# Inverse roots on GpSimd, and degree scaling folded into the adjacency, in a four-layer graph network kernel

## The chip, the cores and the metric

The kernel runs on one core of a Trainium2 chip. The core has five engines with queues of their own: TensorE (PE in the profile, with its weight loads as PEld), VectorE (DVE), ScalarE (ACT), GpSimd (POOL) and SyncE (SP), which here only issues DMAs. Each engine takes its instructions in order. The metric is the device time of one execution in microseconds; the median of three runs of the kernel before is 5732.73 us (5721.88 to 5733.99).

## What is computed

There are 64 graphs of 256 nodes with 128 features and a 0/1 adjacency. Each goes through four layers, and after each layer the input is added and the rows are normalised (mean and variance over the features).

```python
# layer 0: p[i] + q[j] + b, relu, masked by the adjacency, maximum over j
# layer 1: three elu projections, two aggregations with adj and adj^T, tanh of a linear map
# layer 2
A_hat = adj + eye;  deg = A_hat.sum(-1);  dinv = where(deg > 0, rsqrt(deg), 0)
norm_A = dinv[:, None] * A_hat * dinv[None, :]
h = elu(elu(x @ W0 + b0))
h = elu(norm_A @ (h @ W1) + b1)
out = norm_A @ (h @ W2) + b2
# layer 3: for every edge (i, j): layernorm(m_j + m_i + b1), exact gelu, summed over j,
#          then a linear map, a layernorm with gain and bias
x = layernorm(x + layer(x))          # after each of the four
```

Inverse square roots occur in three places: in every layernorm (five per graph, one value for each node), in `dinv` (one value for each node), and in layer 3, where each edge has its own variance and so its own inverse root.

## The kernel before

A graph's 256 nodes lie on the partitions in two halves (H = 2 tiles of 128 rows). Layers 0 and 3 work on edges. The kernel sorts the nodes by degree and packs the edges into "slots" of falling width; the `WIDTH` columns of a half are cut into five tiles of up to 1024 columns (`TILES`), so that one graph has ten edge tiles in layer 3 (`TODO`).

Four stages form a software pipeline over the graphs: `first` (the packing and layer 0), `second` (layer 1), `third` (layer 2, then the first four edge tiles of layer 3) and `last` (the rest of layer 3 and the output). In each of 67 steps, `together` interleaves four stages of four successive graphs: the stages are Python generators, and a `yield` is a point at which another stage may put its instructions in. The order on each engine then comes from the framework's scheduler, which starts from this order and moves instructions by their dependencies and by its own costs. All 64 graphs are unrolled. A second path, `general`, is built behind a run-time test and isn't executed with these inputs.

The lines that matter here:

- `inverse_root` (L72 to L75): a ScalarE square root in place, then a VectorE reciprocal in place. It has three users.
- `Shared.layernorm` (L166): VectorE takes statistics (L171, L172) and adds the epsilon (L174); after a `yield` the root follows, after another the normalisation (L180, or L184 and L185).
- `Shared.layer_2` (L261): it takes the degrees, adds one, makes the mask `pos` and the root `dinv` (L265 to L274), and adds the identity to the transposed adjacency `aT` (L277). In each of its two aggregation steps VectorE multiplies the features `hs` by `dinv` (L293, one instruction per half), TensorE multiplies by `aT` (L296), ScalarE copies (L299), TensorE applies the weights (L304), and L308 multiplies the result's rows by `dinv` and adds the bias.
- `sums_of` (L718), for each edge tile: TensorE gathers (L728), VectorE adds (L732), ScalarE squares (L736), TensorE sums over the features (L743), ScalarE scales into `row` with the epsilon (L745), and a DMA writes `row` to a `line` in DRAM (L750). For each two tiles a DMA brings `line` back spread over the partitions as `vr` (128 or 108 partitions by 16, L762), another brings the mask `fu` (L764); `vr` gets its inverse root (L768) and is multiplied by the mask (L769), and a DMA writes it to DRAM as `scale_line` (L771).
- `last` fetches each tile's scales, broadcast to all partitions, as `rs_s` (L828, two tiles ahead), multiplies with them (L839), applies Gelu (L841) and folds the result into `sums` (L492).
- All DMAs are issued from SP's one queue. A DMA in it that waits for an engine holds back the DMAs behind it.
- ScalarE holds one set of activation functions at a time; the built program has a table load (ACT_TABLE_LOAD, put down to the line of the activation behind it) where the next function isn't in the set that is loaded. Sqrt, Exp and Gelu alternate in this kernel. Copy, Square, Identity, Sign and others need no load.

Of the kernel before, what the change touches and what calls it, by code (L numbers as in the profile page):

```python
# [9 lines left out]
F32 = mybir.dt.float32  # L10
BF16 = mybir.dt.bfloat16
AF = mybir.ActivationFunctionType
ALU = mybir.AluOpType
# [6 lines left out]
P = 128  # L20
EPS = 1e-5
# [22 lines left out]
def kernel(  # L44
# [9 lines left out]
    nc = tc.nc  # L54
    B, N, D = x.shape
    assert N == 2 * P and D == P
    H = N // P
    Q = P // 4

    consts = ctx.enter_context(tc.tile_pool(name="consts", bufs=1))  # L60
# [6 lines left out]
    eps_t = consts.tile([P, 1], F32, name="eps_t")  # L67
    nc.vector.memset(eps_t, EPS)
    minus1 = consts.tile([P, 1], F32, name="minus1")
    nc.vector.memset(minus1, -1.0)  # L70

    def inverse_root(t):  # L72

        nc.scalar.activation(t, t, AF.Sqrt)  # L74
        nc.vector.reciprocal(t, t)  # L75

    def load(src, shape, name):
        t = consts.tile(shape, F32, name=name)
# [43 lines left out]
    with tc.tile_pool(name="prep", bufs=1) as prep, tc.tile_pool(  # L122
        name="ps_prep", bufs=2, space=bass.MemoryType.PSUM
# [33 lines left out]
    class Shared:  # L157
# [8 lines left out]
        def layernorm(self, dst, src, g=None, be=None):  # L166

            st = self.work.tile([P, H, 6], F32, name="st", bufs=4)
            mv = self.work.tile([P, H, 2], F32, name="mv", bufs=4)
            for h in range(H):  # L170
                nc.vector.bn_stats(st[:, h], src[:, h])  # L171
                nc.vector.bn_aggr(mv[:, h], st[:, h])  # L172
            rs = self.work.tile([P, H], F32, name="rs", bufs=4)
            nc.vector.tensor_scalar(rs, mv[:, :, 1], EPS, None, ALU.add)  # L174
            yield
            inverse_root(rs)
            yield
            for h in range(H):
                if g is None:
                    nc.vector.tensor_scalar(  # L180
                        dst[:, h], src[:, h], mv[:, h, 0:1], rs[:, h:h + 1], ALU.subtract, ALU.mult
                    )
                else:
                    nc.vector.scalar_tensor_tensor(dst[:, h], src[:, h], mv[:, h, 0:1], g, ALU.subtract, ALU.mult)  # L184
                    nc.vector.scalar_tensor_tensor(dst[:, h], dst[:, h], rs[:, h:h + 1], be, ALU.mult, ALU.add)  # L185
# [17 lines left out]
        def to_features(self, xn, name, bufs=None):  # L203

            pt = self.psum()
            for h in range(H):
                nc.tensor.transpose(pt[:, h * P:(h + 1) * P], xn[:, h], ident)
            t = self.state.tile([P, N], F32, name=name, **({"bufs": bufs} if bufs else {}))
            nc.scalar.copy(t, pt[:, :N])
            return t  # L210

        def node_tile(self, name):
            return self.state.tile([P, H, P], F32, name=name)
# [44 lines left out]
            yield from self.layernorm(x2, y)  # L258
            s["x2"] = x2

        def layer_2(self, s, aT, deg_of):  # L261

            work, psum, elu = self.work, self.psum, self.elu
            x2 = s["x2"]
            deg = work.tile([P, H], F32, name="deg")  # L265
            deg_of(deg)
            nc.vector.tensor_scalar(deg, deg, 1.0, None, ALU.add)
            pos = work.tile([P, H], F32, name="pos")
            nc.vector.tensor_scalar(pos, deg, 0.0, None, ALU.is_gt)
            dinv = work.tile([P, H], F32, name="dinv")  # L270
            nc.vector.tensor_scalar(dinv, deg, 1e-30, None, ALU.max)
            inverse_root(dinv)
            yield
            nc.vector.tensor_mul(dinv, dinv, pos)  # L274
            for h in range(H):
                blk = aT[:, h, h * P:(h + 1) * P]
                nc.vector.tensor_add(blk, blk, ident)  # L277
            yield
            xT = self.to_features(x2, "xT_2", 1)
            yield  # L280
            ph = psum()
            hs = work.tile([P, H, P], F32, name="hs")
            for h in range(H):
                cols = slice(h * P, (h + 1) * P)
                nc.tensor.matmul(ph[:, cols], xT[:, cols], w2[0], start=True, stop=True)
            yield
            for h in range(H):
                nc.vector.tensor_add(hs[:, h], ph[:, h * P:(h + 1) * P], b2[0])
            yield from elu(hs, hs, twice=True)
            yield  # L290
            for step in (1, 2):
                for h in range(H):
                    nc.vector.tensor_scalar(hs[:, h], hs[:, h], dinv[:, h:h + 1], None, ALU.mult)  # L293
                pa = psum()
                for h in range(H):
                    nc.tensor.matmul(pa[:, :N], hs[:, h], aT[:, h], start=h == 0, stop=h == H - 1)  # L296
                yield
                agg = work.tile([P, N], F32, name="agg")
                nc.scalar.copy(agg, pa[:, :N])  # L299
                yield  # L300
                po = psum()
                for h in range(H):
                    cols = slice(h * P, (h + 1) * P)
                    nc.tensor.matmul(po[:, cols], agg[:, cols], w2[step], start=True, stop=True)  # L304
                yield
                hs = work.tile([P, H, P], F32, name="hs")
                for h in range(H):
                    nc.vector.scalar_tensor_tensor(  # L308
                        hs[:, h], po[:, h * P:(h + 1) * P], dinv[:, h:h + 1], b2[step], ALU.mult, ALU.add
                    )  # L310
                if step == 1:
                    yield from elu(hs, hs)
                yield
            nc.vector.tensor_add(hs, hs, x2)
            x3 = self.node_tile("x3")
            yield from self.layernorm(x3, hs)
            s["x3"] = x3
# [36 lines left out]
    def sparse(ctx):  # L354
# [35 lines left out]
        with tc.tile_pool(name="cs_prep", bufs=1) as pp:  # L390
            t = pp.tile([P, P], F32, name="upto_f")
# [4 lines left out]
            t = pp.tile([P, N], I32, name="iota_i")  # L396
            nc.gpsimd.iota(t, pattern=[[1, N]], base=0, channel_multiplier=0)
            nc.vector.tensor_copy(iota_k, t)
            t = pp.tile([P, 1], I32, name="part_i")
# [25 lines left out]
            t = pp.tile([P, 1], F32, name="gbe")  # L425
# [9 lines left out]
            for i in range(3):  # L435
                t = pp.tile([3, P], BF16, name="u_part")
# [5 lines left out]
            t = pp.tile([ROWS, g_n, g_w], F32, name="tail_f")  # L442
# [7 lines left out]
        state = ctx.enter_context(tc.tile_pool(name="state", bufs=2))  # L450
        hold = ctx.enter_context(tc.tile_pool(name="hold", bufs=4))
        pair = ctx.enter_context(tc.tile_pool(name="pair", bufs=1))
        work = ctx.enter_context(tc.tile_pool(name="work", bufs=1))
        big = ctx.enter_context(tc.tile_pool(name="big", bufs=2))
        sh = Shared(work, state, ps_mm)
# [46 lines left out]
        def first(g, s):  # L502
# [37 lines left out]
            nc.scalar.activation(diff, diff, AF.Abs, accum_out=fl[:, 0:1])  # L540
            kc = work.tile([P, H, H], F32, name="kc")
            nc.vector.scalar_tensor_tensor(kc, pc, -1.0, down_c, ALU.mult, ALU.subtract)
            dg = state.tile([P, H], F32, name="dg", bufs=3)
            nc.vector.tensor_reduce(dg, pc, AX.X, ALU.add)
            s["dg"] = dg

            more = work.tile([P, H, H], F32, name="more")
            for h in range(H):
# [169 lines left out]
        def sums_of(s, i):  # L718

            h, t0, tl = TODO[i]  # L720
# [45 lines left out]
                s["fulls"].rearrange("h w -> (h w)")[first_at:first_at + n].rearrange("(p k) -> p k", k=PIECE),  # L766
            )
            inverse_root(vr[:rows])  # L768
            nc.vector.tensor_mul(vr[:rows], vr[:rows], fu[:rows])  # L769
            out_line = dram.tile([1, GROUP * TILE], F32, name="scale_line")  # L770
            nc.sync.dma_start(out_line[:, :n].rearrange("o (p k) -> (o p) k", k=PIECE), vr[:rows])  # L771
            at = 0
# [8 lines left out]

        def third(g, s):

            dg = s["dg"]

            def deg_of(deg):
                nc.vector.tensor_scalar(deg, dg, 1.0 / N, None, ALU.mult)

            yield from sh.layer_2(s, s["aT"], deg_of)
            yield  # L790
            x3, perm = s["x3"], s["perm"]

            x3T = sh.to_features(x3, "x3T")
            yield
            pc = psum()
            for h in range(H):
                nc.tensor.matmul(
                    pc[:, h * N:(h + 1) * N], x3T[:, h * P:(h + 1) * P], w3c.rearrange("p c o -> p (c o)"),
                    start=True, stop=True,
                )  # L800
            pcv = pc.rearrange("p (h c o) -> p h c o", h=H, c=2)
            dn = work.tile([P, H, P], F32, name="dn")
            nc.scalar.copy(dn, pcv[:, :, 1])
            c3 = state.tile([P, 3, H, P], BF16, name="c3")
            split3(c3, pcv[:, :, 0])
            yield
            pd = psum()
            for h in range(H):
                for hi in range(H):
                    nc.tensor.matmul(  # L810
                        pd[:, h * N:(h + 1) * N], dn[:, hi], perm[:, h, hi], start=hi == 0, stop=hi == H - 1
                    )
            yield
            dT = state.tile([P, H, N], F32, name="dT")
            nc.scalar.activation(dT, pd.rearrange("p (h n) -> p h n", h=H), AF.Identity, bias=b3c)
            s.update(x3T=x3T, c3=c3, dT=dT)
            yield
            for i in range(AHEAD):
                yield from sums_of(s, i)
# [75 lines left out]
    def general(ctx):  # L895
# [82 lines left out]
        def middle(g, s):  # L978
# [7 lines left out]
                nc.scalar.copy(aT[:, hj], pt[:, :N])  # L986
            yield

            def deg_of(deg):
                nc.vector.tensor_reduce(deg, an, AX.X, ALU.add)  # L990

            yield from sh.layer_1(s, an, aT, s["x1"])
            yield
            yield from sh.layer_2(s, aT, deg_of)
            yield

            x3T = sh.to_features(s["x3"], "x3T")
# [145 lines left out]
```

## Time and profile before

| | busy us | share of the span | instructions |
|---|---|---|---|
| TensorE matmul | 4529.9 | 79% | 27408 |
| VectorE | 4834.4 | 84% | 14654 |
| ScalarE | 4275.2 | 75% | 6485 |
| GpSimd | 1.9 | 0% | 10 |

The profiled execution took 5731.62 us, and its span is 5729.7 us; its mean granted TensorE clock is 0.862 of full speed. The table loads of ScalarE are groups of their own: 535 before Gelu (L841), 445 before Sqrt (L74), 221 and 32 before Exp (L194, L198), two before Tanh (L254) and one in the preamble (L426), each 1283 ns. The DMA engines are busy for about a fifth of the span.

A row of a group names line, engine and operation, output and inputs, shapes, count, then busy time in all and mean duration of one, then the engine's idle time just ahead of these instructions and what ended it. The chain is followed back from the last instruction, at each step to what released it.

### The profile page before, as it was taken

To read this page: it belongs to the slowest core of one execution; us is meant where nothing else is said; L and a number is where in the kernel's file an instruction comes from. 1 tells how busy PE (TensorE), PEld (TensorE's weight loads), DVE (VectorE), ACT (ScalarE), POOL (GpSimd) and SP (SyncE) were. 2 spreads that over 40 slices of the span, in tenths; PEclk is the share of its full clock that TensorE was granted. 3 is DMA by queue.
4 is the path that set the end of the run, shared out by engine and by line. 5 is a ranking of instruction groups with operands and counts; after the bars stand their busy time and mean duration, and the time that the engine had idled before them with its cause. 6 is when DMAs were issued, how large, how long until landed. Compare 5 with 4: busy or idle time off the path is not lost.

```text
span 5729.7 us, 83531 instructions
## 1 busy us (share of the span) xinstructions
PE 4529.9 (79%) x27408; PEld 2508.7 (44%) x27408; DVE 4834.4 (84%) x14654; ACT 4275.2 (75%) x6485; POOL 1.9 (0%) x10
## 2 busy tenths in 40 slices
PE   5878878878778778788788788787887887877875
PEld 2444444444444444444444444444444444444443
DVE  6788888888888888888888888888888888888876
ACT  2577777777777777777777777777777777777785
POOL 0000000000000000000000000000000000000000
PEclk8888889889889889888898898898888887888986
DMA  0122222222212221221221222122212212221222
GB/s 22 44 70 63 62 63 72 62 63 66 69 57 70 65 63 63 72 63 62 63 72 62 63 65 70 59 68 65 63 62 72 64 62 63 69 66 60 68 65 74
DMA packets 292813, 365.15 MB, mean 64 GB/s; under 512 B 151952, under 2 KB 210448, under 8 KB 292368
## 3 DMA queue, kind: packets, MB, share of 16 engines
q1 hardware_dynamic: 292368, 359.73, 20.0%
q8 instruction: 217, 3.56, 0.3%
q14 instruction: 228, 1.87, 0.1%
HBM read 345.07 MB, written 14.53 MB: 63 GB/s over the span
## 4 chain that ended last, share of the span: by engine, by line
PE 52%; DVE 29%; ACT 11%; issue 4%; DMA 3%; SPq 0%; DVEq 0%; POOL 0%; ACTq 0%
PE bigp L665 11%; PE bigp L728 8%; DVE pre L839 6%; PE mm L860 5%; DVE lanes L492 4%; PE mm L743 4%; DVE hot L629 4%; DVE pre L732 4%; DVE sums L492 3%; PE bigp L681 3%; DMA rs_s<-scale_line 2%; PE mm L870 2%; PE mm L296 2%; PE mm L699 2%; PE mm L647 2%
## 5 line engine op out<-in xcount | busy, mean ns | idle before, releaser
L665 PE MATMUL bigp<-hot,q 128*128 128x512 fp8e4 (+1 forms) x3840 | 1052.3, 371 | 66.6 <-DVE lanes L492 52.6
L728 PE MATMUL bigp<-hot,c 128*128 128x512 fp8e4 (+1 forms) x3840 | 928.8, 372 | 140.2 <-DVE pre L732 140.2
L732 DVE TENSOR_TENSOR pre<-bigp,dT 128x512 f32<-128x512 f32 (+6 forms) x1664 | 846.3, 530 | 37.8 <-PE bigp L728 33.5
L492 DVE TENSOR_TENSOR lanes<-bigp,lanes 128x512 f32<-128x512 f32 (+6 forms) x1536 | 772.7, 503 | 94.6 <-PE bigp L681 86.9
L839 DVE TENSOR_TENSOR pre<-pre,rs_s 128x1024 f32<-128x1024 f32 (+1 forms) x640 | 732.9, 1150 | 48.6 <-DMA rs_s<-scale_line 48.0
L736 ACT ACTIVATE sq<-pre 128x1024 f32<-128x1024 f32 (+1 forms) x640 | 638.5, 998 | 169.9 <-DVE pre L732 163.9
L841 ACT ACT_TABLE_LOAD x535 | 686.4, 1283 | 9.5
L492 DVE TENSOR_TENSOR sums<-pre,sums 128x1024 f32<-128x1024 f32 (+6 forms) x1024 | 628.8, 614 | 41.2 <-ACT pre L841 40.7
L745 ACT ACTIVATE row<-mm,eps_t 128x256 f32<-128x256 f32 (+1 forms) x640 | 289.6, 453 | 476.9 <-PE mm L743 476.7
L841 ACT ACTIVATE pre<-pre,be,g 128x1024 f32<-128x1024 f32 (+1 forms) x512 | 594.2, 1172 | 57.8 <-DVE pre L839 53.0
L743 PE MATMUL mm<-sq,ones 128*32 128x256 f32 (+1 forms) x5120 | 482.9, 440 | 135.2 <-ACT sq L736 135.2
L74 ACT ACT_TABLE_LOAD x445 | 570.9, 1283 | 7.5
L728 PEld LDWEIGHTS <-c 128*128 128x128 bf16 x3840 | 331.2, 98 | 550.5 <-issue 136.1
L665 PEld LDWEIGHTS <-q 128*128 128x128 bf16 x3840 | 310.8, 97 | 392.6 <-issue 112.0
L296 PE MATMUL mm<-aT,hs 128*128 128x256 f32 x512 | 232.3, 600 | 316.1 <-DVE hs L293 214.8
L629 DVE TENSOR_SCALAR hot<-rank 128x512 fp8e4<-128x512 bf16 (+5 forms) x1536 | 440.5, 348 | 0.0
L681 PEld LDWEIGHTS <-pick 42*128 42x128 bf16 x2944 | 155.8, 95 | 481.5 <-issue 474.2
L296 PEld LDWEIGHTS mm<-aT,hs 128*128 128x128 f32 x512 | 135.6, 293 | 425.8 <-issue 316.1
L860 PE MATMUL mm<-w3u,sums 128*128 128x128 f32 x2048 | 296.7, 289 | 18.4 <-DVE sums L492 16.1
L194 ACT ACT_TABLE_LOAD x221 | 283.5, 1283 | 3.9
L681 PE MATMUL bigp<-lack,pick 42*128 42x36 bf16 (+16 forms) x2944 | 285.7, 187 | 0.0
L860 PEld LDWEIGHTS mm<-w3u,sums 128*128 128x128 f32 x2048 | 254.5, 195 | 37.3 <-issue 17.6
(226 smaller groups left out, 7132.6 us busy)
## 6 DMA issues: line engine op xcount, KB each, us to landing
rs_s<-scale_line SPq DMA_DIRECT2D x512, 512.0 KB
rs_s<-scale_line SPq DMA_DIRECT2D x128, 352.0 KB
an<-in_adj SPq DMA_DIRECT2D x64, 256.0 KB
x<-in_x SPq DMA_DIRECT2D x64, 128.0 KB
line<-row SPq DMA_DIRECT2D x512, 4.0 KB
out<-o SPq DMA_DIRECT2D x64, 128.0 KB
fu<-fulls SPq DMA_DIRECT2D x192, 4.0 KB
vr<-line SPq DMA_DIRECT2D x192, 8.0 KB
```

The lines of the kernel that those rows point to most:

```text
L74: nc.scalar.activation(t, t, AF.Sqrt)
L492: nc.vector.tensor_tensor(lanes[:, :k, :w], src[:, i:i + k], lanes[:, :k, :w], op)
L629: nc.vector.tensor_scalar(hot[:, :, at:at + w], rank[:, :, :w], s0 + i + 1.0 - FAR, None, ALU.is_equal, saturate=False)
L665: nc.tensor.matmul(pt[:, :tl], q3[:, i, h], hot[:, h, t0:t0 + tl], start=i == 0, stop=False)
L681: nc.tensor.matmul(o_, l_, r_, start=False, stop=i == len(todo) - 1)
L728: nc.tensor.matmul(pt[:, :bl], c3[:, k, h], hot[:, h, t0 + b:t0 + b + bl], start=k == 0, stop=k == 2)
L732: nc.vector.tensor_add(block(pre[:, b:], n, w, at), block(pt, n, w, at), widen(dT[:, h, :w], n))
L736: nc.scalar.activation(sq[:, :tl], pre[:, :tl], AF.Square)
L743: nc.tensor.matmul(pr[q * Q:(q + 1) * Q, :tl // 4], ones[:, :Q], v4[:, :, q], start=True, stop=True)
L839: nc.vector.tensor_mul(pre[:, :tl], pre[:, :tl], rs[:, :tl])
L841: nc.scalar.activation(msg[:, :tl], pre[:, :tl], AF.Gelu, bias=be3, scale=g3)
L860: nc.tensor.matmul(pt[:, cols], lanes[:, k, cols], w3u[:, 1], start=k == 0, stop=False)
```

## The change

- `inverse_root` becomes one GpSimd instruction, a power with exponents from a constant tile `mhalf` of -0.5. Its users are now the edge scales `vr` and `dinv`; the multiplications by the masks that follow (`fu`, `pos`) go to GpSimd too.
- The layernorm has its own root: ScalarE's square root reads the variances directly and adds the epsilon as its bias. The reciprocal moves behind the second `yield`, just ahead of the normalisation.
- `dinv` is made in stage `first`, where the degrees are computed, and kept in a state tile with four buffers; before, the degrees were kept in one with three.
- Layer 2 multiplies the rows of `aT`, with the identity added, by `dinv` once for both aggregation steps. The two multiplications of `hs` in each step go.

```diff
+    mhalf = consts.tile([P, 16], F32, name="mhalf")
+    nc.vector.memset(mhalf, -0.5)
     def inverse_root(t):
-        nc.scalar.activation(t, t, AF.Sqrt)
-        nc.vector.reciprocal(t, t)
+        nc.gpsimd.tensor_tensor(t, t, mhalf[:t.shape[0], :t.free_size()], ALU.pow)
@@ layernorm
+            yield
             rs = self.work.tile([P, H], F32, name="rs", bufs=4)
-            nc.vector.tensor_scalar(rs, mv[:, :, 1], EPS, None, ALU.add)
-            yield
-            inverse_root(rs)
-            yield
+            nc.scalar.activation(rs, mv[:, :, 1], AF.Sqrt, bias=eps_t)
+            yield
+            nc.vector.reciprocal(rs, rs)
@@ new in Shared
+        def inverse_root_of(self, deg, bufs):
+            nc.vector.tensor_scalar(deg, deg, 1.0, None, ALU.add)
+            pos = self.work.tile([P, H], F32, name="pos")
+            nc.vector.tensor_scalar(pos, deg, 0.0, None, ALU.is_gt)
+            dinv = self.state.tile([P, H], F32, name="dinv", bufs=bufs)
+            nc.vector.tensor_scalar(dinv, deg, 1e-30, None, ALU.max)
+            inverse_root(dinv)
+            nc.gpsimd.tensor_mul(dinv, dinv, pos)
+            return dinv
@@ layer_2
-            deg = work.tile([P, H], F32, name="deg")
...
-            nc.vector.tensor_mul(dinv, dinv, pos)
+            dinv = dinv_of()
+            yield
             for h in range(H):
                 blk = aT[:, h, h * P:(h + 1) * P]
                 nc.vector.tensor_add(blk, blk, ident)
+            for h in range(H):
+                nc.vector.tensor_scalar(aT[:, h], aT[:, h], dinv[:, h:h + 1], None, ALU.mult)
...
             for step in (1, 2):
-                for h in range(H):
-                    nc.vector.tensor_scalar(hs[:, h], hs[:, h], dinv[:, h:h + 1], None, ALU.mult)
                 pa = psum()
@@ first
-            dg = state.tile([P, H], F32, name="dg", bufs=3)
+            dg = work.tile([P, H], F32, name="dg")
             nc.vector.tensor_reduce(dg, pc, AX.X, ALU.add)
-            s["dg"] = dg
+            nc.vector.tensor_scalar(dg, dg, 1.0 / N, None, ALU.mult)
+            s["dinv"] = sh.inverse_root_of(dg, 4)
@@ sums_of
             inverse_root(vr[:rows])
-            nc.vector.tensor_mul(vr[:rows], vr[:rows], fu[:rows])
+            nc.gpsimd.tensor_mul(vr[:rows], vr[:rows], fu[:rows])
```

More of the change, by code (lines that the diff above doesn't have):

```diff
@@ L259, in layer_1, with layer_2 @@
             s["x2"] = x2
-        def layer_2(self, s, aT, deg_of):
+        def layer_2(self, s, aT, dinv_of):
             work, psum, elu = self.work, self.psum, self.elu
             x2 = s["x2"]
-            deg = work.tile([P, H], F32, name="deg")
[L266 to L272, printed above, removed]
+            dinv = dinv_of()
             yield
-            nc.vector.tensor_mul(dinv, dinv, pos)
             for h in range(H):
@@ L782, in third @@
         def third(g, s):
[L784 to L789, printed above, removed]
+            yield from sh.layer_2(s, s["aT"], lambda: s["dinv"])
             yield
@@ L987, in middle, with dinv_of @@
             yield
-            def deg_of(deg):
+            def dinv_of():
+                deg = work.tile([P, H], F32, name="deg")
                 nc.vector.tensor_reduce(deg, an, AX.X, ALU.add)
+                return sh.inverse_root_of(deg, 1)
             yield from sh.layer_1(s, an, aT, s["x1"])
             yield
-            yield from sh.layer_2(s, aT, deg_of)
+            yield from sh.layer_2(s, aT, dinv_of)
             yield
```

## The prediction

> **What bounds the kernel now.** I read the busy times first.
>
> ```profile
> PE 4529.9 (79%) x27408; PEld 2508.7 (44%) x27408; DVE 4834.4 (84%) x14654; ACT 4275.2 (75%) x6485; POOL 1.9 (0%) x10
> ```
>
> No engine is full, and three are close to it: the steps are limited by engines that wait for each other in order. The chain of waits says the same.
>
> ```profile
> PE 52%; DVE 29%; ACT 11%; issue 4%; DMA 3%; SPq 0%; DVEq 0%; POOL 0%; ACTq 0%
> ```
>
> TensorE has half of the path, and the change leaves its work alone. VectorE and ScalarE have 40%, and there it cuts. The groups of instructions price what goes.
>
> ```profile
> L841 ACT ACT_TABLE_LOAD x535 | 686.4, 1283 | 9.5
> L74 ACT ACT_TABLE_LOAD x445 | 570.9, 1283 | 7.5
> L194 ACT ACT_TABLE_LOAD x221 | 283.5, 1283 | 3.9
> ...
> L75 DVE RECIPROCAL vr<-vr 128x16 f32<-128x16 f32 (+1 forms) x320 | 78.4, 245 | 29.5 <-ACT vr L74 25.4
> L560 DVE TENSOR_SCALAR perm<-iota_k,place 128x256 f32<-128x256 f32 x256 | 72.7, 347 | 0.1
> L293 DVE TENSOR_SCALAR hs<-hs,dinv 128x128 f32<-128x128 f32 x256 | 61.0, 270 | 2.2
> L769 DVE TENSOR_TENSOR vr<-vr,fu 128x16 f32<-128x16 f32 (+1 forms) x320 | 52.9, 165 | 0.3
> L174 DVE TENSOR_SCALAR rs<-mv 128x2 f32<-128x2 f32 x320 | 51.1, 160 | 0.1
> ```
>
> More than a third of ScalarE's busy time is table loads (1236 of 1283 ns, 1586 us). The timeline of ScalarE in one step shows them alternating where nothing but table switches separates the work:
>
> ```profile
> 3020.31 1.28 ACT L194 ACT_TABLE_LOAD   x1
> 3021.60 0.63 ACT L194 ACTIVATE elu_e<-io 128x512 f32<-128x512 f32 x1
> 3022.25 1.28 ACT L74 ACT_TABLE_LOAD   x1
> 3023.55 0.21 ACT L74 ACTIVATE vr<-vr 108x16 f32<-108x16 f32 x1
> ...
> 3025.36 1.28 ACT L194 ACT_TABLE_LOAD   x1
> ```
>
> A root of 0.21 us costs two loads. Last, the waits at the places that the change touches:
>
> ```profile
> PE mm L296 <- DVE hs L293: 214.8, 67, 8.7
> ...
> DVE pre L839 <- DMA rs_s<-scale_line: 48.0, 57, 4.2
> ```
>
> So the edge scales sometimes arrive just too late, and the layer-2 products wait for VectorE.
>
> **What the Trainium skill says.** "ScalarE: Activation LUTs", section What ACT_TABLE_LOAD costs, gives about 1283 ns for a load of any set; the trace agrees to the digit. "VectorE: DVE Perf Modes", section Mode 2×_2P, says that an fp32 multiplication by a scalar within SBUF takes two elements a cycle through both read ports; the trace agrees: L200 takes 289 ns for 256 columns and 415 ns for 512, so 0.49 ns more per column. "SBUF — State Buffer", section Who interferes with whom, says that the second port pair is shared with GpSimd and locked: a VectorE instruction in such a mode, or with two SBUF inputs, and a GpSimd instruction that reads SBUF exclude each other for a whole instruction. No line of the kernel before shows it, since GpSimd has ten instructions, all in the preamble. This lock is the main risk.
>
> **The change part by part.**
>
> *Table loads and roots on ScalarE.* In the changed program as built, the executed path has 767 loads in place of 1236: Gelu 535 to 379, Sqrt 445 to 195, Exp 253 to 191 (both lines). 469 × 1.283 = 602 us of ScalarE, and 384 roots × about 0.21 = 81 us: 683 us less. On the path, counted by adding the chain's pieces line by line: loads before L74 48.1 us, before L194 89.4, L198 39.7, L841 12.8. Scaled by the share of each that goes (250/445, 32/221, 30/32, 156/535): 27 + 13 + 37 + 4 = 81 us. The roots of `vr` have 8 on it. Together 89.
>
> *VectorE, removed:* reciprocals of `vr` 78.4 and `dinv` 9.4, masks 52.9 and 6.4, epsilon 51.1, L293 61.0: 259 us. *Added:* 128 multiplications of `aT`, 128×256, priced between L200's 289 and L560's 347 ns; I take 320: 41 us. Net 218 us less busy. On the chain stand L174 22, `vr` L75 22, L293 14, L769 10: 68; the addition at VectorE's share of the path (0.29/0.84 = 35%) takes back 14. Net 54.
>
> *The scale's way.* From the issue of the DMA that brings `vr` to the issue of the one that takes `scale_line` away, five groups of one step took 5.73, 8.05, 5.98, 3.73 and 5.18 us, mean 5.73. In the shortest the root began 2.91 us after the issue, right behind a ScalarE copy, so 2.9 is an upper estimate of the DMA. The root, reciprocal and mask take 0.62; the rest, 2.2 us, is queueing behind other work of ScalarE and VectorE. After the change it is 2.9 + power + mask on an engine with nothing else to do. The mask on GpSimd: "GPSIMD Engine Reference", section 3.1, gives 2.6 cycles per element for two inputs at 1.2 GHz, so 16 elements are 0.04 us plus a fixed part; the preamble's GpSimd instructions (386 and 450 ns for 128 and 192 columns) bound it from above; I take 0.2. The power has no price on a page and no row. Below, it can't be under the mask's 0.2. Above: section 7 of the same page gives 4 cycles for each link of a dependent fp32 chain; 20 to 60 links for a logarithm and an exponential (my guess at the number) are 80 to 240 cycles per element, 1.1 to 3.2 us for 16. I take 1.3. Then the way is 4.4 us, 1.3 shorter. The chain runs through `rs_s` DMAs 32 times and `scale_line` DMAs 9 times: 41 × 1.3 = 53 us. With a power of 3.2 it is 23 us longer instead; with 0.2, 100 us shorter.
>
> SP's queue: in the built order `scale_line` comes right behind `vr` in several groups, where before `row` DMAs stood between. SP waits there for GpSimd, and the `row` and `rs_s` issues behind it wait with it; at 4.4 us a group, five groups hold SP for 22 of about 86 us of a step, so I cost it at nothing; at a power over 3 us that cover thins.
>
> *Made in `first`.* `dinv`'s four small VectorE instructions only move, about 40 us of work in both kernels; its root is ready a stage before `aT` needs it. The layernorm's moved reciprocal costs nothing by itself: it stands next to the normalisation, which needs it anyway.
>
> *The port lock.* GpSimd gets 320 × (1.3 + 0.2) + 64 × 0.5 = 512 us of instructions. VectorE work that reads two SBUF tensors or uses two ports: L839 733, `sums` of L492 629, L629 440, and some thirty smaller groups, about 1000: 2800 of 5730 us, 49%. If each GpSimd instruction holds the lock throughout, VectorE loses 512 × 0.49 = 250 us, and at 35% on the path 88 us. If the lock is held only while it reads, next to nothing. I take half, 44.
>
> *Sum.* 89 + 54 + 53 = 196 us off the present path. The step alternates between paths of near length (VectorE's 73 us, TensorE's 71.5 and ScalarE's 65.5 in an 86 us window), so a second one takes over; I keep three quarters, 147. Less 44 of lock: 103 off the profiled execution's 5731.6, so about 5630. The profiled execution and the median of the runs, 5732.7, are 1 us apart, so this holds for the median.
>
> **Rivals.** *GpSimd becomes the brake (slower).* The power takes long and holds the port. With full lock and a power of p us, the balance is −107 (three quarters of 89 + 54) + 0.17 × (320 × (p + 0.2) + 32) + 41 × (p − 2.6); zero at p = 2.1. At 3.2 us it gives +109, so 5840; at 3.6 some 5880. For it: nobody has priced the power, [...]and VectorE is the fullest engine. Against: the tile is only 16 columns. *The relief compounds.* The lock is nothing, and VectorE keeps its 84% at 4616 us of work: 4616 / 0.844 = 5470; with part of it, 5520. For it: ScalarE loses 12% of the span, and it often holds VectorE and TensorE up (L743 waits 135 us for L736, L304 62 us for L299). Against: TensorE's half of the path stays. *Nothing moves.* TensorE's work and the packing's run of L629 take the path wherever it is relieved: 5720 to 5740. Against: loads and `vr` stand on the chain themselves. That the loads don't go can't be: their number is in the built program.
>
> **How the numbers follow.** Likeliest, 5630 (its own range 5550 to 5715): 0.46. Compounding, 5520: 0.14. Brake, around 5840: 0.30. Nothing moves: 0.10. About 0.2% is what a measurement of this kernel can tell. Faster is then 0.46 + 0.14 + 0.02 of the last; same 0.07; slower 0.31. The range drops half of the compounding case and a third of the brake: 5490 to 5880.
>
> **What would show it.** Right: 767 loads and ScalarE near 3600 us busy; VectorE near 4620 plus stretched instructions; `vr` powers of about 1.3 us on GpSimd; L296 waiting less for VectorE; fewer `rs_s` DMAs on the chain. Wrong: powers over 2 us; L839 or L492 `sums` longer than 1216 and 1219 ns at 1024 columns; L839 waiting for `rs_s` far more than 48 us; SP stalled at `scale_line`; a lower granted TensorE clock when its waits shrink.

## The result, and the profile after

The changed kernel takes 5826.45 us, the median of four runs (5820.15 to 5836.14); the kernel before takes 5729.03 us beside it (5721.88 to 5733.99). The ratio is 1.0172 with a 95% interval of 1.0153 to 1.0192: 97 us slower, where 103 us faster was forecast. The time lies inside the range that was given, near the 5840 us of the rival "GpSimd becomes the brake".

The first view is the busy times of the changed kernel, in the same columns as the line shown of the kernel before.

```profile
PE 4572.8 (78%) x27408; PEld 2549.1 (44%) x27408; DVE 4697.2 (81%) x13439; ACT 3683.1 (63%) x5632; POOL 1237.5 (21%) x778
```

The work did go away: ScalarE is 592 us less busy and VectorE 137 us, and the run is longer all the same. The table loads are down to 767, as counted ahead, and no engine is as full as VectorE was. So the loss is mostly waiting, not work. TensorE alone is busier, by 43 us for the same 27408 matmuls, at a mean granted clock of 0.844 against 0.862; what that is worth is looked at below, at the half power. The new work is on GpSimd; its two dearest groups, and the load groups of ScalarE, read:

```profile
L77 POOL TENSOR_TENSOR vr<-vr,mhalf 128x16 f32<-128x16 f32 (+1 forms) x320 | 1025.6, 3205 | 4302.0 <-DMA vr<-line 4302.0
...
L842 ACT ACT_TABLE_LOAD x379 | 486.3, 1283 | 6.7
...
L177 ACT ACT_TABLE_LOAD x195 | 250.2, 1283 | 3.5
...
L196 ACT ACT_TABLE_LOAD x189 | 242.5, 1283 | 3.4
...
L775 POOL TENSOR_TENSOR vr<-vr,fu 128x16 f32<-128x16 f32 (+1 forms) x320 | 151.3, 473 | 25.1
```

One power over 16 columns takes 3205 ns in the mean (shortest 2898, median 2902, longest 3994). The mask takes 217 ns at its shortest, 218 in the median, and 473 in the mean.

Next the waits, in the order engine, waiting line, what released it, then total, number of times and longest. The chain of waits of this kernel can't be used: its chain breaks off at the end of the program.

```profile
PE mm L572 <- DVE perm L566: 365.5, 64, 7.5
DVE pre L840 <- DMA rs_s<-scale_line: 308.0, 87, 5.8
...
DVE rest L503 <- ACT q L502: 187.5, 62, 3.1
```

The second is the change's own: VectorE's multiplication of an edge tile by its scales (L840, L839 before) waits 308 us for them, against 48. The other two are old waits that grew: TensorE's for `perm` was 245.5 us, VectorE's for `q` 93.4 us.

The instructions of VectorE themselves did not get longer. These are its groups of 1024 columns in the changed kernel, the shapes kept apart; both read two tensors in SBUF:

```profile
L840 DVE TENSOR_TENSOR pre<-pre,rs_s 128x1024 f32<-128x1024 f32 x512 | 622.0, 1215 | 297.5 <-DMA rs_s<-scale_line 297.4
...
L497 DVE TENSOR_TENSOR sums<-pre,sums 128x1024 f32<-128x1024 f32 x256 | 311.3, 1216 | 82.5 <-ACT pre L842 82.3
```

They took 1216 and 1219 ns before. Whatever the shared port does, it is not these VectorE instructions that are stretched.

**Where the 308 us lie.** Added up by edge tile over the 64 graphs, 270 us of the wait are at tile 2, in 63 of the 64 graphs; before, tile 2 waited 1.3 us in all, and the largest sum of any tile was 26 us. Tiles 2 and 3 share one group of scales, made at the end of stage `third` and used near the beginning of `last`. From the issue of the DMA that brings this group's `vr` to the issue of the one that takes its `scale_line` away it takes 6.87 us in the mean, against 4.92 before. The groups of tiles 0 and 1, 4 and 5, 6 and 7, and 8 and 9 went from 4.07, 5.91, 7.63, 5.91 us to 5.12, 6.17, 7.53, 5.07. So four of five ways changed by about a microsecond or less, and the one that decides became 1.95 us longer.

The timeline of one step shows it: time, duration, engine, line, and in brackets the idle time just ahead. First GpSimd, then SyncE.

```profile
3040.08 3.62 POOL L77 TENSOR_TENSOR vr<-vr,mhalf 128x16 f32<-128x16 f32 x1 [12.59 <-DMA vr<-line]
3043.78 1.34 POOL L775 TENSOR_TENSOR vr<-vr,fu 128x16 f32<-128x16 f32 x1
...
3045.15 0.32 SPq L777 DMA_DIRECT2D scale_line<-vr  x1
3045.51 0.43 SPq L770 DMA_DIRECT2D fu<-fulls  x1
3046.59 0.79 SPq L829 DMA_DIRECT2D rs_s<-scale_line  x2
```

Then VectorE in the same microseconds:

```profile
3039.74 1.21 DVE L840 TENSOR_TENSOR pre<-pre,rs_s 128x1024 f32<-128x1024 f32 x1
3042.13 0.59 DVE L182 TENSOR_SCALAR x<-y,mv,rs 128x128 f32<-128x128 f32 x2
3043.84 1.21 DVE L497 TENSOR_TENSOR sums<-pre,sums 128x1024 f32<-128x1024 f32 x1
3046.04 0.16 DVE L220 TENSOR_SCALAR dinv<-dg 128x2 f32<-128x2 f32 x1
3050.67 1.22 DVE L840 TENSOR_TENSOR pre<-pre,rs_s 128x1024 f32<-128x1024 f32 x1 [4.47 <-DMA rs_s<-scale_line]
3051.82 0.48 DVE L295 TENSOR_TENSOR hs<-mm,b 128x128 f32<-128x128 f32 x2
3052.21 0.74 DVE L239 TENSOR_TENSOR io<-mm,b_io 128x256 f32<-128x256 f32 x2
```

Three things are to be seen. The power took 3.62 us here, 0.72 more than its shortest: it was issued while L840, with two inputs in SBUF, ran until 3040.95. That is the rule in this group: 60 of its 64 powers began during an L840, and each ended 2.76 to 2.83 us after that L840 did. The mask took 1.34 instead of 0.22: it ended at 3045.12, right after the `sums` of L497, which began 0.06 us behind it and ended at 3045.05. Of this group's 64 masks, 59 ended so, 0.07 to 0.08 us after such a sum. And VectorE stood still for 4.47 us, with `hs` and `io` queued behind the multiplication that waited.

That last point is a change of order. The same place in the kernel before reads:

```profile
3005.94 0.76 DVE L226 TENSOR_TENSOR io<-mm,b_io 128x256 f32<-128x256 f32 x2 [2.84 <-PE mm L223]
3006.79 0.49 DVE L288 TENSOR_TENSOR hs<-mm,b 128x128 f32<-128x128 f32 x2
3007.20 2.45 DVE L839 TENSOR_TENSOR pre<-pre,rs_s 128x1024 f32<-128x1024 f32 x2
```

SyncE's queue just before these lines reads:

```profile
2999.50 0.33 SPq L771 DMA_DIRECT2D scale_line<-vr  x1
...
3000.96 0.32 SPq L828 DMA_DIRECT2D rs_s<-scale_line  x1
```

Before, `io` and `hs` go first and the multiplications follow. The fetch of the scales comes 1.46 us after `scale_line` here and 1.44 us after it in the changed step, so that part of the way is as it was. But the multiplication starts 7.70 us after `scale_line` here and 5.52 us after it there. Over all graphs the medians are 7.53 and 5.54 us, and 5.53 us is what it takes when the multiplication waits: the kernel before had about 2 us to spare at tile 2. In the changed program the scheduler has put tile 2's multiplication ahead of both. The elus of layers 1 and 2 and their next products wait for `io` and `hs`, so what VectorE loses there goes on to ScalarE and TensorE.

### The profile page after: what moved, and what is told of

The parts are those of the page before. It is cut to its first block, busy times and chain, and to the rows that moved or that the text cites. A ratio compares the mean times of both kernels' runs of the same rounds, so it can differ in the third digit from the quotient of the medians.

```text
span 5826.1 us, 82183 instructions
## 1 busy us (share of the span) xinstructions
PE 4572.8 (78%) x27408; PEld 2549.1 (44%) x27408; DVE 4697.2 (81%) x13439; ACT 3683.1 (63%) x5632; POOL 1237.5 (21%) x778
## 5 line engine op out<-in xcount | busy, mean ns | idle before, releaser
L77 POOL TENSOR_TENSOR vr<-vr,mhalf 128x16 f32<-128x16 f32 (+1 forms) x320 | 1025.6, 3205 | 4302.0 <-DMA vr<-line 4302.0
L671 PE MATMUL bigp<-hot,q 128*128 128x512 fp8e4 (+1 forms) x3840 | 1023.8, 370 | 57.9 <-DVE lanes L497 46.0
L840 DVE TENSOR_TENSOR pre<-pre,rs_s 128x1024 f32<-128x1024 f32 (+1 forms) x640 | 734.4, 1148 | 308.2 <-DMA rs_s<-scale_line 308.0
L497 DVE TENSOR_TENSOR lanes<-bigp,lanes 128x512 f32<-128x512 f32 (+6 forms) x1536 | 773.8, 504 | 147.4 <-PE bigp L687 136.6
L497 DVE TENSOR_TENSOR sums<-pre,sums 128x1024 f32<-128x1024 f32 (+6 forms) x1024 | 626.6, 612 | 86.8 <-ACT pre L842 86.2
L301 PE MATMUL mm<-aT,hs 128*128 128x256 f32 x512 | 254.8, 651 | 160.7 <-DVE hs L203 160.7
L572 PE MATMUL mm<-perm,nz 128*128 128x256 bf16 x256 | 74.4, 377 | 365.5 <-DVE perm L566 365.5
L687 PE MATMUL bigp<-lack,pick 42*128 42x36 bf16 (+16 forms) x2944 | 316.5, 188 | 0.0
L301 PEld LDWEIGHTS mm<-aT,hs 128*128 128x128 f32 x512 | 149.0, 321 | 278.8 <-issue 240.8
```

The lines of the kernel that those rows point to most:

```text
L77: nc.gpsimd.tensor_tensor(t, t, mhalf[:t.shape[0], :t.free_size()], ALU.pow)
L497: nc.vector.tensor_tensor(lanes[:, :k, :w], src[:, i:i + k], lanes[:, :k, :w], op)
L671: nc.tensor.matmul(pt[:, :tl], q3[:, i, h], hot[:, h, t0:t0 + tl], start=i == 0, stop=False)
L687: nc.tensor.matmul(o_, l_, r_, start=False, stop=i == len(todo) - 1)
L840: nc.vector.tensor_mul(pre[:, :tl], pre[:, :tl], rs[:, :tl])
```

## The experiments

The kernel before was measured beside each of them; its median was about 5727 us. "Wait for the scales" means the wait of `last`'s multiplication for `rs_s`, as in the waits above; "way" is from the `vr` DMA's issue to the `scale_line` DMA's, for the group of tiles 2 and 3.

### A root that costs almost nothing, in the same program

```diff
-            inverse_root(vr[:rows])
+            nc.gpsimd.tensor_tensor(vr[:rows], vr[:rows], mhalf[:rows, :PIECE], ALU.mult)
```

> The changed kernel with the power of the edge scales replaced by a multiplication on GpSimd (same operands, same order on every engine; the edge scales are then not inverse roots). Theory A, the power's duration makes the scales of the third edge tile late (270 us of VectorE's waits at that tile): GpSimd's instruction falls from 2.9 to about 0.2 us, 64 x 2.7 = 173 us of that wait go, so about 5655, and VectorE's wait for the scales is back under 100 us in all. Rival B, the scheduler's new order of the other engines' instructions costs the time: the order is unchanged here, so 5815 to 5835. Rival C, the port that GpSimd and VectorE share: gain like A's, but shorter VectorE instructions would have to show it.

Measured: 5636.36 us (5634.64 to 5640.7), ratio 0.9844 [0.9827, 0.986]. The instructions have the same order on every engine as in the changed kernel; only the length of one of GpSimd's is another. GpSimd's group and VectorE's wait:

```profile
L774 POOL TENSOR_TENSOR vr<-vr,mhalf 128x16 f32<-128x16 f32 (+1 forms) x320 | 154.6, 483 | 4721.9 <-DMA vr<-line 4721.9
```

```profile
DVE pre L840 <- DMA rs_s<-scale_line: 45.0, 55, 4.8
```

The way is 3.16 us. Theory A comes out, near its 5655 us and with a wait under 100 us, and rival B's forecast fails: in one and the same order the power's length costs 190 us and turns the sign. Rival C, as it was put, fails too: VectorE's instructions would have to be shorter, and VectorE is as busy as in the changed kernel (4705.6 against 4697.2 us). So is TensorE (4568.3 against 4572.8 us). With this short instruction (0.48 us in the mean) in the power's place the change gains 90 us.

### Half of the power

```diff
-            inverse_root(vr[:rows])
+            nc.gpsimd.tensor_tensor(vr[:rows, :8], vr[:rows, :8], mhalf[:rows, :8], ALU.pow)
```

> The changed kernel with the power over 8 of the 16 columns of an edge-scale group (the other half of the scales stays variances; same order on every engine). Dose between the changed kernel (2.9 us) and the multiplication (0.2 us): by 0.70 us for 2 columns and 2.90 for 16, 8 columns take 1.64. Theory A, lateness: 64 x 1.26 = 81 us of the wait at the third tile go, 190 remain, so about 5745 (5720 to 5770). If lateness has a threshold only, 5800 or more, or 5650 or less.

Measured: 5673.89 us (5669.68 to 5679.56), ratio 0.9908 [0.9891, 0.9924], again in the same order. That is faster than theory A's 5720 to 5770. The power over 8 columns takes 1892 ns in the mean.

```profile
DVE pre L840 <- DMA rs_s<-scale_line: 138.2, 71, 5.2
```

Tile 2 waits 122 us, the way is 4.63 us, and this group's mask is back at 0.22 us where it took 1.26 in the mean. With the two kernels beside it this is a dose: tile 2's wait of 30, 122 and 270 us goes with 5636, 5674 and 5826 us. The second half of the power costs four times the first (152 against 38 us); a part of the first is slack. It also speaks on order: the way is shorter here than before (4.92 us), and tile 2 still waits 1.9 us a graph, because its multiplication stands early.

This run settles another rival, the clock. Its mean granted TensorE clock is 0.843, as low as the changed kernel's 0.844, and TensorE is even a little busier (4607.7 against 4572.8 us); yet it takes 152 us less. So the lower clock isn't the cause of the 190 us. What the 43 us of TensorE are worth beside the kernel before is not measured.

### The old root for all edge scales

```diff
-            inverse_root(vr[:rows])
-            nc.gpsimd.tensor_mul(vr[:rows], vr[:rows], fu[:rows])
+            nc.scalar.activation(vr[:rows], vr[:rows], AF.Sqrt)
+            nc.vector.reciprocal(vr[:rows], vr[:rows])
+            nc.vector.tensor_mul(vr[:rows], vr[:rows], fu[:rows])
```

> The changed kernel with root, reciprocal and mask of the edge scales all back on ScalarE and VectorE; dinv early on GpSimd, layernorm and layer 2 as changed (built table loads 1085 instead of 767 and 1236). Theory A: the other parts are a small gain: 151 loads fewer than before and about 87 us less of VectorE, so 5650 to 5710. Rival D: they are a loss, 5740 to 5850.

Measured: 5715.55 us (5711.09 to 5719.99), ratio 0.9982 [0.9972, 0.9991]. The wait for the scales is 15.6 us, and ScalarE has 1085 loads. That is a little above theory A's 5650 to 5710. The rest of the change, the layernorm's root, `dinv` and layer 2 together, is worth some 11 us in this order. By difference, about 80 of the 90 us would come with the edge scales' root, once it leaves ScalarE and VectorE; but the two kernels differ in order too, and the runs on layer 2 below show how much an order can be worth, so this split is not shown.

### The power alone, in the kernel before

```diff
+    mhalf = consts.tile([P, 16], F32, name="mhalf")
+    nc.vector.memset(mhalf, -0.5)
...
-            inverse_root(vr[:rows])
-            nc.vector.tensor_mul(vr[:rows], vr[:rows], fu[:rows])
+            nc.gpsimd.tensor_tensor(vr[:rows], vr[:rows], mhalf[:rows, :PIECE], ALU.pow)
+            nc.gpsimd.tensor_mul(vr[:rows], vr[:rows], fu[:rows])
```

> The kernel before with one part of the change alone: root and mask of the edge scales on GpSimd (dinv and layernorms stay on ScalarE, layer 2 as before; built table loads 767). Theory A: this part alone brings the loss, so 5800 to 5900, with 200 to 300 us of VectorE waiting for scales. Rival D, another part of the change (the adjacency's multiplication, the layernorm's later reciprocal) brings it: near or below 5730.

Measured: 5916.51 us (5911.84 to 5926.16), ratio 1.0336 [1.0318, 1.0354].

```profile
DVE pre L842 <- DMA rs_s<-scale_line: 606.6, 146, 6.4
```

That is 190 us slower than the kernel before, 469 table loads fewer and all, and slower than either theory said; that it is 190 us as above is a coincidence, since the power's cost and the gain of the loads are in one sum here. Tile 2 waits 311 us, in every graph, and tile 4 waits 273 us. Tile 2's multiplication stands ahead of `hs` and `io` here as in the changed kernel: moving the root is enough for the scheduler to choose that order.

### The masks back on VectorE

```diff
-            nc.gpsimd.tensor_mul(vr[:rows], vr[:rows], fu[:rows])
+            nc.vector.tensor_mul(vr[:rows], vr[:rows], fu[:rows])
```

> The changed kernel with the masks of the edge scales back on VectorE, powers on GpSimd. GpSimd's mask takes 1.26 us in the late group against 0.22 free, so if waiting for the shared port there is part of the lateness, the way is 0.5 to 0.9 us shorter and the wait at the third tile 30 to 60 us less, while VectorE has 53 us more to do: 5790 to 5830. If it isn't, the crossing back to VectorE costs: 5830 to 5870.

Measured: 5980.73 us (5974.6 to 5988.07), ratio 1.0442 [1.0424, 1.0459]. Neither expectation holds.

```profile
DVE vr L775 <- POOL vr L77: 547.2, 315, 4.2
```

The wait for the scales is gone (11 us at tile 2), and the program has 647 loads instead of 767; but VectorE stands in its own queue until GpSimd's power is done, 315 times. A mask on VectorE puts the power's whole length in VectorE's order of work for every group, where the DMA's delay had reached it for one group in five. So this run can't say what the mask's own delay at the port costs.

### Tile 2's multiplication two steps later

```diff
                     h, t0, tl = TODO[i]
+                    if i == 2:
+                        yield
+                        yield
                     pre, rs = s.pop(("pre", i)), scale_of.pop(i)
```

> The changed kernel with two more yields ahead of the third edge tile's multiplication in the stage last: in the built order VectorE then takes layer 1's and layer 2's additions (io, hs) and one more tile's sums ahead of this multiplication, as it took io and hs in the kernel before; all powers stay on GpSimd. Theory A2, the loss is the power's duration together with the new place of the multiplication in VectorE's queue: the wait at the third tile falls from 270 to under 120 us, time 5640 to 5740. Theory A1, the place doesn't matter, the scales are late for whatever comes next: 5790 or more.

Measured: 6139.73 us (6128.53 to 6144.28), ratio 1.0721 [1.0703, 1.0739].

```profile
DVE pre L843 <- DMA rs_s<-scale_line: 657.9, 297, 6.4
```

Tile 2's wait fell to 96 us, but the two yields move the whole stage `last`, not one instruction: tile 4 waits 333 us, tile 8 137, tile 0 44, and the program has 882 loads instead of 767. It was meant to settle what the place of the multiplication costs apart from the length of the way, and it doesn't: its time can't be read for either theory.

### The old root for the one late group

```diff
-            inverse_root(vr[:rows])
-            nc.gpsimd.tensor_mul(vr[:rows], vr[:rows], fu[:rows])
+            if i == AHEAD - 1:
+                nc.scalar.activation(vr[:rows], vr[:rows], AF.Sqrt)
+                nc.vector.reciprocal(vr[:rows], vr[:rows])
+                nc.vector.tensor_mul(vr[:rows], vr[:rows], fu[:rows])
+            else:
+                inverse_root(vr[:rows])
+                nc.gpsimd.tensor_mul(vr[:rows], vr[:rows], fu[:rows])
```

> The changed kernel with the root of one of the five edge-scale groups of a graph (tiles 2 and 3) back on ScalarE and its reciprocal and mask on VectorE; the other four stay on GpSimd. Theory A, lateness of this one group: nearly all of the loss goes, wait at the third tile from 270 to under 60 us, time 5600 to 5690, faster than the kernel before. Rival C, GpSimd's use of the shared port: four fifths of the powers remain, so four fifths of the loss: 5790 or more. Rival B, order: the order changes a little, so no sharp forecast, 5780 to 5830.

Measured: 5645.73 us (5643.82 to 5650.74), ratio 0.986 [0.9844, 0.9877]. Only the group of tiles 2 and 3 goes the old way; the other four keep the power of 3.0 us.

```profile
DVE pre L845 <- DMA rs_s<-scale_line: 38.5, 26, 5.7
```

```profile
L775 ACT ACTIVATE vr<-vr x64: 197/199/217, 197.3 to 5580.9; 128x16 f32<-128x16 f32 x64
L775 ACT ACT_TABLE_LOAD  x1: 1283/1283/1283, 196.0 to 196.0; - x1
```

The second fence is the record of that line on ScalarE (shortest, median and longest in ns). One table load in 64 roots: this root falls where Sqrt is loaded already, and the program keeps 767 loads. Theory A's forecast holds and rival C's fails. The run is 181 us faster than the changed kernel, with four of the five powers as long as they were: in this order their length costs little. The order is another one, though, with tile 2's multiplication behind `io` and `hs` again, and the clock is higher (0.877 against 0.844, with TensorE 64 us less busy), so the gain is that of the shorter way, of the order and perhaps of the clock together. This version beats both kernels, by 1.4% and 3.1%.

### Layer 2 as before, and the layernorm as before

Four runs undo one other part, each on a kernel above. In the first three the rows of `aT` aren't multiplied and `hs` is multiplied in each step:

```diff
-            for h in range(H):
-                nc.vector.tensor_scalar(aT[:, h], aT[:, h], dinv[:, h:h + 1], None, ALU.mult)
...
             for step in (1, 2):
+                for h in range(H):
+                    nc.vector.tensor_scalar(hs[:, h], hs[:, h], dinv[:, h:h + 1], None, ALU.mult)
                 pa = psum()
```

On the kernel with the old root for the late group:

> The kernel of the run with one group's root on ScalarE (e2, 5646 us), with layer 2's part undone: features multiplied twice, adjacency not multiplied. If that part gains what VectorE saves there (61.0 - 38.9 = 22 us) and shortens the way to the products, 5660 to 5705; if it is hidden, 5640 to 5655.

Measured: 5987.04 us (5982.43 to 5997.68), ratio 1.0453 [1.0436, 1.0471]; 341 us more than without this edit.

```profile
DVE pre L845 <- DMA rs_s<-scale_line: 389.0, 166, 6.3
```

That is no price of two multiplications. The order changed, and now tile 4 waits, 265 us over all 64 graphs, and tile 8 102 us: the powers of other groups come on the path as soon as another order has their scales wanted earlier.

On the kernel with the root that costs almost nothing, where no scale is late for a power:

> The kernel of e1 (multiplication in place of the power, so the edge scales are not inverse roots; 5636 us) with layer 2's part undone: features multiplied twice, adjacency not. VectorE has 61.0 - 38.9 = 22 us more. No late scales can disturb here. Theory E, layer 2's part gains by taking two instructions out of the way to the products: 5660 to 5720. Theory F, it is hidden and the 5987 us of e8 came from another group's late scales: 5630 to 5660.

Measured: 5630.33 us (5627.31 to 5638.34), ratio 0.9836 [0.982, 0.9853], beside 5636.36. Layer 2's part gains nothing in this order, as theory F said. And its waits warn against adding waits up:

```profile
DVE pre L840 <- DMA rs_s<-scale_line: 219.6, 115, 4.8
```

It is a wait of 220 us, 180 of it at tile 4, in a kernel that is no slower. What a wait costs depends on what is queued behind it.

On the kernel with the old root for all edge scales:

> The kernel of e4 (edge-scale roots on ScalarE; 5716 us) with layer 2's part undone in the same way; the scheduler then places 1146 table loads instead of 1085. Theory E: 5740 to 5800, Theory F: 5705 to 5735.

Measured: 5808.32 us (5806.71 to 5811.53), ratio 1.0149 [1.0132, 1.0166], 93 us more than the 5715.55 without the edit and above both theories; 61 more loads.

```profile
PE mm L301 <- DVE hs L298: 394.0, 127, 8.3
```

There TensorE waits 394 us for `hs`, against 188.7. The last two disagree, 6 us less against 93 us more for the same edit, so the value of layer 2's part is a matter of the order around it; what in the order decides stays open. The first of the two has a slightly higher clock than its kernel (0.863 against 0.857), the second a lower one (0.849 against 0.868), which may be part of it.

The layernorm's edit was undone on the kernel with the old root for all edge scales:

```diff
-            yield
             rs = self.work.tile([P, H], F32, name="rs", bufs=4)
-            nc.scalar.activation(rs, mv[:, :, 1], AF.Sqrt, bias=eps_t)
+            nc.vector.tensor_scalar(rs, mv[:, :, 1], EPS, None, ALU.add)
             yield
+            nc.scalar.activation(rs, rs, AF.Sqrt)
             nc.vector.reciprocal(rs, rs)
+            yield
```

> The kernel of e4 (5716 us) with the layernorm's part undone: epsilon added by VectorE, reciprocal ahead of the second yield. If the 51 us of VectorE that this part saves count at VectorE's share of the path (35%), 5730 to 5740; if the added pointer operand of ScalarE's root (293 instead of 201 ns) and the later reciprocal take it back, 5705 to 5720.

Measured: 5761.76 us (5753.34 to 5772.33), ratio 1.0067 [1.0046, 1.0088]: 46 us more than the 5715.55, above both forecasts, with 1083 loads against 1085. So it isn't the loads that this part saves there; VectorE is 55 us less busy with it (4767.2 against 4822.5). The 46 us of this part and the 93 us of layer 2's can't be added: all the parts together gained 11 us.

## Why the prediction was wrong

**The scale's way** is the step that failed, in its size and in its form. The size: it took the power at 1.3 us, from its bounds of 0.2 and 3.2; it is 2.90 us alone and 3.2 in the mean, the top of the bound. That made the way of the deciding group 1.95 us longer instead of 1.3 shorter. But the size alone doesn't give a loss. With 3.2 in the prediction's own sum, loads, VectorE and way are (89 + 54 − 23) × 3/4 = 90 us of gain, and the half lock grows to 95 us: about no change. With the lock at nothing for VectorE, which is what the two groups named show, it would still have been 90 us faster. The form is what failed: a mean change of the way, times 41 visits of the chain, as if all groups were alike. The mean of the five ways did move only from 5.69 to 6.15 us, which 41 visits make 19 us; the length of the power cost 190 us, because 270 of the 308 us of wait fall on one group, in 63 of 64 graphs. In the order with the old root for that group the other four bear a power of 3 us.

Looking at the kernel before for the group whose scales are wanted soonest would not have found it: tiles 4 and 8 were multiplied 6.86 and 6.63 us after their `scale_line` in the median, tile 2 only after 7.53. In the changed program its multiplication comes earlier and its scales later, as the views above show.

**The port lock** was costed at 44 us of longer VectorE instructions. None of the two groups named got longer (1215 and 1216 ns). The lock is there, as the Trainium skill's "SBUF — State Buffer", section Who interferes with whom, says of GpSimd and a VectorE instruction with two SBUF inputs: GpSimd's powers and masks of the late group end a fixed time after such an instruction. But in this trace the loser is GpSimd, and its loss lies on the scale's way: in the mean of the late group the power takes 3.59 us and the mask 1.26, which is 0.7 and 1.0 us over their shortest. Nor is it held for the whole of a power: 64 of the L840 multiplications of 1024 columns, with two inputs in SBUF, ran from beginning to end inside a power, in 1.21 to 1.23 us each, as long as without one. The page's block for a whole instruction, on which the prediction's full lock rests, isn't what this trace shows while a power runs. So a part of the failure does come from the port, but as a later end of GpSimd's work; between the half power and the full one the group's way grows by 2.24 us, of which the power is 1.18 and the mask's meeting with a sum 1.03. How many of the 190 us that is, no run separates.

**The order taken as given.** The prediction read the waits and covers of the kernel before and laid the new durations on them. The scheduler put tile 2's multiplication ahead of `hs` and `io`. At the old way of 4.92 us the new order would wait as well, as the half power shows with 1.9 us at 4.63. Of the 4.2 us a graph in the changed kernel, the longer way then makes some 2 and the place the rest. That split is argued from those two numbers, not shown; the run that was to show it moved too much. In the old order, with its 2 us to spare, the longer way alone might have cost little. The order is fixed in the built program; the prediction drew on it for the loads and for SyncE's queue, not for this.

**The rival that came true** is "GpSimd becomes the brake": slower from a power of 2.1 us on, 5840 us at 3.2. Measured are 3.2 us and 5826. Its place was wrong: 190 us of its sum are VectorE locked out at the port, and what happened is that one group's scales came late. The near number is chance.

**Right** were the 767 loads and, roughly, ScalarE's relief: 592 us against 683 forecast, of which some 30 are the layernorm's roots, 0.09 us longer with the epsilon as bias in each of 320. TensorE waits less for VectorE at the layer-2 products, 160.7 us against 214.8. That the kernel takes 5636 us with a root of almost no cost, near the forecast 5630, is luck: 5630 was for a power of 1.3 us. For 0.2 us the prediction's terms give, as an estimate, (89 + 54 + 100) × 3/4 less 14 of lock, 168 us of gain, and 90 were measured. So the relief was taken too high, by nearly half.

**VectorE's busy time** fell by 137 us, not by the 218 reckoned. The busy times of its rows add up to 5654 us before and 5405 after, so they did fall by 249; but in all it was busy for 4834 and 4697 us. In the timelines small instructions begin before their neighbours end, by some tens of ns, so 1215 of them fewer free less than their rows say.

**SP's queue** and **made in `first`** were costed at nothing. SyncE held the late group's `scale_line` until the mask was done at 3045.12; that wait is part of the way above. No run separates either of the two.

## What to carry to other kernels

An instruction that no row and no page prices is to be taken at the top of its bound when it goes on a way with a deadline, or measured alone first; here the top of the bound was the answer. A relief of a busy engine counts only if no group's data arrive later than its consumer can bear, so ask for each consumer, not in the mean, and read the built order for what is queued behind it. Where one consumer of five is tight, the slow operation can stay off that one: the old root for one group kept all 469 saved table loads and made 5646 us of 5826. Which consumer is tight is a matter of the order, and another edit can move it, as layer 2's did (5987 us).

## What the runs showed of the hardware

GpSimd's power over fp32 takes 0.70 us for 2 columns (the row of `dinv`, 696 ns), 1.64 us for 8 and 2.90 for 16 at the shortest: about 0.157 us a column and 0.38 us fixed. A multiplication of two tensors on the same 16 columns takes 0.22 us. A GpSimd power or mask that meets a VectorE instruction with two SBUF inputs ends later (a mask at 1.34 us), while such a VectorE instruction inside a running power keeps its 1.21 us. A root on ScalarE with the epsilon as its bias takes 0.29 us where it took 0.20 without.
